# A selective scan that spreads B in fp32, with zero products in TensorE's gaps and fewer products on VectorE

## The chip, the cores and the metric

The kernel runs on one core of a Trainium2 chip. The metric is the time of one execution on the device, in microseconds (us). A core has TensorE (PE, matrix products into PSUM; PEld is its weight load), VectorE (DVE), ScalarE (ACT), GpSimd (POOL) and SyncE (SP), which here only issues transfers. The engines run beside each other and wait for each other through semaphores.

## The reference

The network takes x of shape 4 x 56 x 56 x 96 through two layers that hold a selective scan (a state-space model, run along the image in four directions) and then two attention layers. The scan takes nearly all of the time. For each image and direction, with 192 channels d, 16 states n and 3136 tokens t:

```python
dt   = softplus(...)                    # per token and channel
d_a  = exp(dt[..., None] * a)           # decay, per token, channel and state
d_b  = dt[..., None] * b_ssm[:, :, None, :]

def step(h, inp):
    da_t, db_t, x_t, c_t = inp
    h = da_t * h + db_t * x_t[..., None]     # the recurrence
    y_t = jnp.einsum('bds,bs->bd', h, c_t)   # sum over the states
    return (h, y_t)
```

The rows of B and C (`b_ssm`, `c_ssm`) and the input of dt are linear projections of the same token. Layer norms, convolutions, gates and small matrix products lie before, between and after the scans.

## The kernel before

Tokens are worked in chunks of 448. There are 2 layers x 4 images x 4 directions x 7 chunks = 224 chunks, and each chunk has 8 rounds: two halves `e` of the channels times four groups `q` of states, so 1792 rounds. In a round, 128 partitions hold 4 states x 32 channels, and three blocks `g` of 448 tokens hold the three groups of 32 channels.

The projection gives rows of C and B in 64 of 128 partitions, and a second copy of them in the other 64. GpSimd makes that copy the remainder beyond bf16, so that one bf16 product over 128 rows gives B nearly in fp32:

```python
def rows(self, ch):                      # ScalarE copies the projection out of PSUM
    ...
    ch.cf = sp.tile([128, CS], F32, name="cf")
    ...
def spread_b(self, ch, q):               # B of four states, on 32 partitions each
    ps = self.psum.tile([128, 512], F32, tag="b", name="b", bufs=1)[:, :CS]
    self.nc.tensor.matmul(ps, self.sel[:, q], self.upper(ch.cf), start=True, stop=True)
    return ps

def split(self, ch, n):                  # the remainder, in two parts, in rounds 1 and 2
    x = ch.cf[64 + 32 * n :]
    self.nc.gpsimd.tensor_tensor(x, x, self.upper(x), ALU.subtract)
```

`upper` is the high half of each fp32 word, read as bf16. `b` has one buffer, so the next B waits until VectorE's products have read the last one. A round, cut to what matters:

```python
def begin(n):
    ch, e, q = rounds[n]
    b = self.spread_b(ch, q)
    v = sp.tile([128, NG, CS + 2], F32, name="v", bufs=3)
    ahead = NQ * e + q not in (OWN_TAIL if ch.l and ch.i else OWN)
    if ahead:                            # GpSimd makes the third block's product
        nc.gpsimd.tensor_tensor(v[:, 2, TOKENS], ch.du[e][:, 2], ch.cb[q][:, 1], ALU.mult)
    return b, v, ahead
...
for n, (ch, e, q) in enumerate(rounds):
    b, v, ahead = nxt
    for g in range(2 if ahead else 3):   # VectorE makes two products, or all three
        nc.vector.tensor_tensor(v[:, g, TOKENS], ch.du[e][:, g], b, ALU.mult)
    self.prepare(ch, nexts.get(ch), r)   # parts of the next chunk
    ...
    yield "C", n, r                      # side work: the other layers' pieces
    nxt = begin(n + 1)
    if len(late) == 2:
        self.add_up(*late.pop(0))        # the sum over states, two rounds late
    self.prepare_ahead(afters.get(ch), r)
    for g in range(NG):
        ...                              # before g == 2: more side work
        nc.vector.tensor_tensor_scan(    # the recurrence of 448 tokens
            v[:, g, way], da[g][:, way], v[:, g, way], 0.0, ALU.mult, ALU.add)
        ...
        decay(n + 1, g)                  # ScalarE: exp(dt * a) of the next round into PSUM
    hc = sp.tile([128, NG, CS], F32, name="hc", bufs=3)
    nc.gpsimd.tensor_tensor(hc, v[:, :, TOKENS],   # h times C
        ch.cb[q][:, 0].unsqueeze(1).to_broadcast([128, NG, CS]), ALU.mult)
    late.append((ch, e, q, hc))
```

`add_up` sums over the four states of a partition group with four matrix products of 32 columns each (the fourth is a spare whose rows are not used):

```python
for n, g in enumerate((0, 1, 2, 2)):
    nc.tensor.matmul(self.y[32 * n : 32 * n + 32], self.four, hc[:, g], start=n == 3, stop=n == 3 or q == NQ - 1)
```

`OWN = (3, 4, 6)` are the rounds of a chunk in which VectorE makes all three products; `OWN_TAIL = (3, 4)` replaces it in the second layer from the second image on. Side work (norms, convolutions, gates, attention of the other images) is cut into pieces, and each piece goes into a round when an account of estimated ScalarE and TensorE time, `spend` and `room`, has room for it. The order of instructions on each engine is fixed when the program is built.

Of the kernel before, what the change touches and what calls it, by code (L numbers as in the profile page):

```python
# [11 lines left out]
F32 = mybir.dt.float32  # L12
F16 = mybir.dt.float16
BF16 = mybir.dt.bfloat16
F8 = mybir.dt.float8e5
AF = mybir.ActivationFunctionType
ALU = mybir.AluOpType
# [5 lines left out]
C = 96  # L23
DI = 192
NS = 16
NE = 2
NG = 3
NQ = 4
# [7 lines left out]
RANK = (12, 6)  # L36
NW, LATE_NW = 13, 20
NWIN = 3
OWN = (3, 4, 6)
OWN_TAIL = (3, 4)  # L40

SPARE = (1.2, 3.0)
# [2 lines left out]
BANKS, LATE_BANKS = 2, 4  # L45
DEPTH, LATE_DEPTH = 3, 6

ORDER = (((0, 0), (0, 1), (1, 0), (1, 1)), ((0, 1), (1, 0), (1, 1), (0, 0)))
WD = NE * 128 + NE * C + NE + NE * NQ * NG

# [29 lines left out]
def lay_out(i):  # L82
    i = {k: np.asarray(v) for k, v in i.items()}
    c96, c128, w96, w128, q96, q128 = Cols(C), Cols(128), Cols(C), Cols(128), Cols(C), Cols(128)
    p0, p1 = "L0_conv_", "L1_conv_"

    for n in ("norm_w", "norm_b", "norm2_w", "norm2_b", "ffn_b2"):
        c96.add("0" + n, i[p0 + n][:, None])
    for n in (
        "dw_b bn1_g bn1_b bn1_m bn1_v pw_b bn2_g bn2_b bn2_m bn2_v ln_g ln_b fus_b fus_ln_g fus_ln_b"  # L90
    ).split():
        c96.add("1" + n, i[p1 + n][:, None])
    c96.add("1dw_w", i[p1 + "dw_w"].reshape(C, 9))
    for l in "23":
        c96.add(l + "bq", i[f"L{l}_attn_bqkv"][:C, None])
        c96.add(l + "bff", i[f"L{l}_attn_bff"][:, None])
        c96.add(l + "b2", i[f"L{l}_ffn_b2"][:, None])
        c128.add(l + "b1", i[f"L{l}_ffn_b1"].reshape(3, 128).T)

    scan = (  # L100
        (i[p0 + "ssm_xw"], i[p0 + "ssm_dtw"], i[p0 + "ssm_dtb"], i[p0 + "ssm_Alog"], i[p0 + "ssm_D"]),
        (
            i[p1 + "x_proj_w"],
            i[p1 + "dt_w"],
            i[p1 + "dt_b"],
            i[p1 + "A_logs"].reshape(4, DI, NS),
            i[p1 + "Ds"].reshape(4, DI),
        ),
    )
    wd = np.zeros((2, 4, 128, WD), np.float32)  # L110
    for l, (xw, dw, db, al, dd) in enumerate(scan):
        r = RANK[l]
        for k in range(4):
            t = xw[k].T
            m = np.zeros((128, NE, 2, 64), np.float32)
            m[:C, :, 0, :32] = np.concatenate([t[:, r + NS :], t[:, r : r + NS]], 1).reshape(NE, C, 32).swapaxes(0, 1)
            m[:C, :, 0, 32 : 32 + r] = t[:, :r].reshape(NE, C, r).swapaxes(0, 1)
            m[:, :, 1, :32] = m[:, :, 1, 32:] = m[:, :, 0, :32]
            wt = np.zeros((128, DI), np.float32)
            wt[32 : 32 + r] = dw[k].T  # L120
            bias = np.zeros((128, NE), np.float32)
            bias[:C] = db[k].reshape(NE, C).T
            a = al[k].reshape(NE, NG, 32, 4, NQ).transpose(3, 2, 0, 4, 1).reshape(128, -1)
            wd[l, k] = np.concatenate([m.reshape(128, -1), wt, bias, a], 1)
        c128.add(f"{l}D", dd.T.reshape(NE, C, 4).swapaxes(0, 1))
    c128.add("0dir", np.broadcast_to(i[p0 + "dir_w"], (128, 4)))
    c128.add("0b1", i[p0 + "ffn_b1"].reshape(3, 128).T)
    for n, v in (
        ("1conv_b", i[p1 + "conv_b"][:, None]),
        ("1conv_w", i[p1 + "conv_w"].reshape(DI, 9)),  # L130
        ("1g", i[p1 + "out_norm_g"][:, None]),
        ("1b", i[p1 + "out_norm_b"][:, None]),
    ):
        c128.add(n + "a", v[:128])
        c128.add(n + "b", v[128:])

    w96.add("0in", _in_blocks(i[p0 + "in_w"].T))
    w96.add("1in", _in_blocks(i[p1 + "in_proj_w"].T))
    w96.add("0w1", i[p0 + "ffn_w1"].T)
    w96.add("1pw", i[p1 + "pw_w"])  # L140
    f = i[p1 + "fus_w"].T
    w96.add("1fa", f[:C])
    w96.add("1fb", f[C:])
    w96.add("1out", i[p1 + "out_proj_w"])
    w = i[p0 + "out_w"].T
    w128.add("0outa", w[:128])
    w128.add("0outb", w[128:])
    w128.add("0w2", i[p0 + "ffn_w2"].T.reshape(3, 128, C).transpose(1, 0, 2))
    for l in "23":
        w96.add(l + "qkv", i[f"L{l}_attn_Wqkv"])  # L150
        w96.add(l + "ff", i[f"L{l}_attn_Wff"])
        q96.add(l + "w1", i[f"L{l}_ffn_W1"].T)
        q128.add(l + "w2", i[f"L{l}_ffn_W2"].T.reshape(3, 128, C).transpose(1, 0, 2))
    bqkv = np.stack([i[f"L{l}_attn_bqkv"] for l in "23"])
    cols = {"c96": c96, "c128": c128, "w96": w96, "w128": w128, "q96": q96, "q128": q128}
    arrays = {"x": np.ascontiguousarray(i["x"]).reshape(NB, L, C), "bqkv": bqkv, "wd": wd}
    arrays.update({k: v.array() for k, v in cols.items()})
    return arrays, {k: v.at for k, v in cols.items()}


class Net:
    def __init__(self, ctx, tc, aps, at, out):
# [10 lines left out]
        self.ready = set()  # L173
        self.held, self.lend, self.live, self.g = 0, 0, [], {}
        self.backlog, self.limit, self.paced = [0.0, 0.0], ACT_LIMIT, False
        self.U = [self.big.tile([C, L], F32, name=f"U{e}") for e in range(NE)]
        self.Y = [self.big.tile([C, L], F32, name=f"Y{e}") for e in range(NE)]
        self.wp = pool("work", bufs=2)
# [63 lines left out]
    def setup(self):  # L242
# [94 lines left out]
        self.b2q = const.tile([C, 2], F32, name="b2q")  # L337
        with tc.tile_pool(name="stage", bufs=1) as st:

            self.sel = const.tile([128, NQ, 128], BF16, name="sel")  # L340
            parts = st.tile([128, 128], F32, name="parts")
            nc.vector.tensor_tensor(parts[:, :32], self.ident[:, 64:96], self.ident[:, 96:], ALU.add)
            nc.vector.tensor_tensor(parts[:, :32], parts[:, :32], self.ident[:, :32], ALU.add)
            for q in range(NQ):
                nc.vector.tensor_copy(
                    self.sel[:, q].rearrange("p (s d) -> p s d", s=4),
                    parts[:, NS + q : NS + q + 13 : 4].unsqueeze(2).to_broadcast([128, 4, 32]),
                )
            t = st.tile([C, 2, 3, 128], F32, name="q96")
            nc.scalar.dma_start(t.rearrange("p l m f -> p (l m f)"), self.aps["q96"])  # L350
            nc.vector.tensor_copy(self.w1q, t, saturate=False)
# [64 lines left out]
    def project_step(self, ch, e):  # L416

        if e == 0:
            ch.ps = self.pp()
        self.nc.tensor.matmul(  # L420
            ch.ps.rearrange("p (a b) -> p a b", b=HS), ch.par.wx[:, e],
            self.in_order(self.U[e], ch.orient, ch.c * CS, CS), start=e == 0, stop=e == NE - 1,
        )

    def parameters(self, ch):

        nc, sp = self.nc, self.sp
        if ch.step == 0:
            self.p = p = Step()
            wd = sp.tile([128, WD], F32, name="wd")  # L430
            nc.sync.dma_start(wd, self.aps["wd"][ch.l, ch.k])
            a = NE * 128
            p.wx = wd[:C, :a].rearrange("p (e m) -> p e m", e=NE)
            p.wt = wd[:, a : a + NE * C]
            a += NE * C
            p.dtb = wd[:C, a : a + NE]
            p.alog = wd[:, a + NE :]
            p.na = sp.tile([128, NE, NQ, NG], F32, name="na")
            p.carry = sp.tile([128, NE, NQ, NG], F32, name="carry")
        ch.par = self.p  # L440
# [10 lines left out]
    def rows(self, ch):  # L451
        nc, sp, p = self.nc, self.sp, ch.par
        if ch.step == 0:
            na = p.na.rearrange("p e q g -> p (e q g)")
            nc.scalar.activation(na, p.alog, AF.Exp)
            nc.scalar.mul(na, na, -1.0)
        ch.cf = sp.tile([128, CS], F32, name="cf")
        if ch.l == 0:
            nc.scalar.activation(ch.cf, ch.ps, AF.Copy, scale=self.cscale[:, ch.k : ch.k + 1])  # L459
        else:  # L460
            nc.scalar.copy(ch.cf, ch.ps)

# [56 lines left out]
    def prepare(self, ch, follow, r):  # L519
# [8 lines left out]
            self.rows(follow)  # L528
        elif r == 1:
            self.step_sizes(follow)  # L530
            self.split(follow, 0)
        elif r == 2:
            self.softplus(follow)
            self.split(follow, 1)
        elif r == 3:
            self.times_u(follow, 0)
            for e in range(NE):
# [21 lines left out]
    def spread_b(self, ch, q):  # L559

        ps = self.psum.tile([128, 512], F32, tag="b", name="b", bufs=1)[:, :CS]
        self.nc.tensor.matmul(ps, self.sel[:, q], self.upper(ch.cf), start=True, stop=True)  # L562
        return ps

    def upper(self, x):

        return x.bitcast(BF16).rearrange("p (t h) -> p t h", h=2)[:, :, 1]

    def split(self, ch, n):

        x = ch.cf[64 + 32 * n :]
        self.nc.gpsimd.tensor_tensor(x, x, self.upper(x), ALU.subtract)  # L575

    def scans(self):

# [115 lines left out]
    def add_up(self, ch, e, q, hc):  # L694

        nc = self.nc
        if q == 0:
            self.y = self.psum.tile([128, 512], F32, tag="y", name="y", bufs=1)[:, :CS]
            o = self.y[:C].rearrange("p (a b) -> p a b", b=HS)
            a, w = (self.U[e], self.skip[ch.l][:, e]) if ch.skip else (self.Y[e], self.ident[:C, :C])  # L700
            nc.tensor.matmul(o, w, self.in_order(a, ch.orient, ch.c * CS, CS), start=True, stop=False)  # L701

        for n, g in enumerate((0, 1, 2, 2)):
            nc.tensor.matmul(  # L704
# [167 lines left out]
            yield  # L872

    def spend(self, act, pe):
        self.backlog = [a + b for a, b in zip(self.backlog, (act, pe))]

    def half_round(self):
# [397 lines left out]
```

## Time and profile before

| | |
|---|---|
| time, median of 3 | 9206.25 us (9201.96 to 9231.71) |
| span of the profiled execution | 9215.2 us |
| mean granted TensorE clock | 0.733 |
| transfers | 1417 MB, 154 GB/s |

Its costliest groups, in the page's form (line, engine, operation, what is written and read, count, then busy us and mean ns of one, then the idle time just before them and what ended most of it):

```profile
L687 POOL TENSOR_TENSOR hc<-v,cb 128x1344 f32<-128x1344 f32 x1792 | 5154.2, 2877 | 619.7 <-DVE v L677 304.7
L677 DVE TENSOR_TENSOR_SCAN v<-da,v 128x449 f32<-128x449 f32 (+1 forms) x5376 | 5480.6, 1071 | 166.3 <-ACT da L624 68.6
L624 ACT ACTIVATE da<-dt,na 128x448 f32<-128x448 f32 x5376 | 3407.4, 638 | 1851.5 <-DVE v L677 1808.7
L704 PE MATMUL y<-hc,four 128*32 128x448 f32 x14336 | 2319.9, 729 | 4.3 <-POOL hc L687 4.0
L562 PE MATMUL b<-cf,sel 128*128 128x448 bf16 x1792 | 809.5, 452 | 814.0 <-DVE v L652 812.0
```

An fp32 product stands in the records as two instructions. The page also gives the busy share of each engine in 40 equal slices of the span, a digit for tenths, and PEclk, the share of full speed that TensorE's clock was granted in the slice.

### The profile page before, as it was taken

The numbers are of one execution on the slowest core, as the hardware profiler recorded it, in microseconds if no ns is written. First come the engines' busy times: TensorE is split into PE (matmuls) and PEld (weight loads), VectorE is DVE, ScalarE is ACT, GpSimd is POOL, SyncE is SP. The second block draws the span as 40 slices with busy tenths as digits, with TensorE's granted clock in tenths as the row PEclk, the third lists the DMA queues.
The fourth block names the chain that finished last, engine by engine and source line by source line (L and its number), as shares of the span: only waits on it lengthen the run. The fifth ranks groups of instructions, "written<-read, shape, count | busy, mean of one in ns | idle before, by whom it ended". The sixth has DMA issues, their size and how long they took to land. (4 is left out here: it accounts for less than half of the span.)

```text
span 9215.2 us, 110220 instructions
## 1 busy us (share of the span) xinstructions
PE 7255.3 (79%) x28342; PEld 2367.6 (26%) x28342; DVE 7878.4 (85%) x10197; ACT 6155.2 (67%) x12259; POOL 7816.4 (85%) x4320
## 2 busy tenths in 40 slices
PE   6777677787778777876778768887888788987887
PEld 2222122221222122221222113322233222322244
DVE  5998988899888998989888997899878998888951
ACT  5777667676777667766776655577755776666645
POOL 5888988899888988889888898899878998888951
PEclk7777677776787677866777667776777777876786
DMA  5666666667666676667656675566755666665631
GB/s 150 171 172 167 169 164 158 154 164 185 153 160 150 162 177 159 164 144 173 170 147 157 154 181 141 129 159 155 178 133 139 156 167 170 148 147 132 163 87 41
DMA packets 951297, 1417.21 MB, mean 154 GB/s; under 512 B 176578, under 2 KB 943812, under 8 KB 949796
## 3 DMA queue, kind: packets, MB, share of 16 engines
q1 hardware_dynamic: 949888, 1408.37, 62.4%
q8 instruction: 223, 3.65, 0.2%
q14 instruction: 414, 3.39, 0.1%
q10 hardware_dynamic: 772, 1.80, 0.1%
HBM read 1141.42 MB, written 268.14 MB: 153 GB/s over the span
## 5 line engine op out<-in xcount | busy, mean ns | idle before, releaser
L687 POOL TENSOR_TENSOR hc<-v,cb 128x1344 f32<-128x1344 f32 x1792 | 5154.2, 2877 | 619.7 <-DVE v L677 304.7
L677 DVE TENSOR_TENSOR_SCAN v<-da,v 128x449 f32<-128x449 f32 (+1 forms) x5376 | 5480.6, 1071 | 166.3 <-ACT da L624 68.6
L624 ACT ACTIVATE da<-dt,na 128x448 f32<-128x448 f32 x5376 | 3407.4, 638 | 1851.5 <-DVE v L677 1808.7
L652 DVE TENSOR_TENSOR v<-du,b 128x448 f32<-128x448 f32 x4172 | 2341.0, 608 | 770.0 <-PE b L562 626.4
L704 PE MATMUL y<-hc,four 128*32 128x448 f32 x14336 | 2319.9, 729 | 4.3 <-POOL hc L687 4.0
L562 PE MATMUL b<-cf,sel 128*128 128x448 bf16 x1792 | 809.5, 452 | 814.0 <-DVE v L652 812.0
L632 POOL TENSOR_TENSOR v<-du,cb 128x448 f32<-128x448 f32 x1204 | 1368.5, 1137 | 81.0 <-DMA cb<-cd 57.3
L704 PEld LDWEIGHTS y<-hc,four 128*32 128x32 f32 x14336 | 319.3, 123 | 1802.8 <-issue 1101.0
L420 PE MATMUL pp<-U,wd 96*128 96x448 f32 x896 | 701.8, 871 | 10.0 <-DMA U<-u 9.9
L751 POOL TENSOR_TENSOR rs<-rs,power 112x4 f32<-112x4 f32 x252 | 253.9, 1008 | 532.8 <-ACT rs L750 341.8
L831 PE MATMUL ps<-win,dg 64*64 64x220 f32 (+10 forms) x1962 | 598.7, 516 | 64.8 <-ACT dtc L485 47.1
L701 PE MATMUL y<-Y,ident 96*96 96x448 f32 x672 | 585.2, 964 | 4.7 <-ACT carry L681 3.0
L491 POOL TENSOR_TENSOR duc<-dtc,U 96x448 f32<-96x448 f32 x448 | 557.0, 1243 | 2.5 <-ACT dtc L485 2.5
L711 ACT COPY Y<-y 96x448 f32<-96x448 f32 x448 | 339.8, 758 | 269.3 <-PE y L704 268.3
L624 ACT ACT_TABLE_LOAD x385 | 494.0, 1283 | 14.7 <-DMA dt<-dd 8.0
L562 PEld LDWEIGHTS <-sel 128*128 128x128 bf16 x1792 | 208.8, 117 | 951.7 <-issue 948.7
L575 POOL TENSOR_TENSOR cf<-cf 64x448 f32<-64x448 f32 x448 | 417.0, 931 | 38.1 <-ACT cf L459 3.0
L755 PE MATMUL ps<-ident,rs 112*96 112x112 f32 x1752 | 304.1, 337 | 181.2 <-POOL rs L751 100.1
L729 PE MATMUL ps<-w,cen 96*96 96x448 f32 x448 | 281.1, 730 | 169.1 <-DVE w L1093 42.8
L681 ACT COPY carry<-v 128x3 f32<-128x3 f32 x1536 | 295.8, 193 | 171.0 <-DVE v L677 168.9
L747 PE MATMUL ps<-avg,w 96*112 96x1 f32 (+2 forms) x1976 | 295.6, 267 | 96.1 <-ACT w L784 46.8
L831 PEld LDWEIGHTS ps<-win,dg 64*64 64x64 f32 (+2 forms) x1962 | 248.6, 178 | 451.9 <-issue 321.2
(411 smaller groups left out, 6328.9 us busy)
## 6 DMA issues: line engine op xcount, KB each, us to landing
cb<-cd SPq DMA_DIRECT2D x3584, 112.0 KB, 4.0
dt<-dd SPq DMA_DIRECT2D x1792, 168.0 KB, 4.2
du<-dd SPq DMA_DIRECT2D x1792, 168.0 KB, 4.0
dd<-dtc SPq DMA_DIRECT2D x448, 168.0 KB, 2.0
dd<-duc SPq DMA_DIRECT2D x448, 168.0 KB, 2.0
U<-u SPq DMA_DIRECT2D x112, 168.0 KB, 4.7
z<-w SPq DMA_DIRECT2D x56, 224.0 KB, 3.6
u<-w SPq DMA_DIRECT2D x56, 224.0 KB, 2.9
```

The source lines that it names most:

```text
L420: self.nc.tensor.matmul(ch.ps.rearrange("p (a b) -> p a b", b=HS), ch.par.wx[:, e], self.in_order(self.U[e], ch.orient, ch.c * CS, CS), st ...
L491: self.nc.gpsimd.tensor_tensor(du.rearrange("p (a b) -> p a b", b=HS), ch.dtc[e].rearrange("p (a b) -> p a b", b=HS), self.in_order(self.U ...
L562: self.nc.tensor.matmul(ps, self.sel[:, q], self.upper(ch.cf), start=True, stop=True)
L575: self.nc.gpsimd.tensor_tensor(x, x, self.upper(x), ALU.subtract)
L624: nc.scalar.activation(da[g][:, TOKENS], ch.dt[e][:, g], AF.Exp, scale=ch.par.na[:, e, q, g : g + 1])
L632: nc.gpsimd.tensor_tensor(v[:, 2, TOKENS], ch.du[e][:, 2], ch.cb[q][:, 1], ALU.mult)
L652: nc.vector.tensor_tensor(v[:, g, TOKENS], ch.du[e][:, g], b, ALU.mult)
L677: nc.vector.tensor_tensor_scan(v[:, g, way], da[g][:, way], v[:, g, way], 0.0, ALU.mult, ALU.add)
L687: nc.gpsimd.tensor_tensor(hc, v[:, :, TOKENS], ch.cb[q][:, 0].unsqueeze(1).to_broadcast([128, NG, CS]), ALU.mult)
L701: nc.tensor.matmul(o, w, self.in_order(a, ch.orient, ch.c * CS, CS), start=True, stop=False)
L704: nc.tensor.matmul(self.y[32 * n : 32 * n + 32], self.four, hc[:, g], start=n == 3, stop=n == 3 or q == NQ - 1,)
L831: self.nc.tensor.matmul(o[:, a - r0 : e - r0, x0:x1], diag[:, tap], win[:, a + dy - lo : e + dy - lo, x0 + dx : x1 + dx], start=n == 0, st ...
```

## The change

It has four parts. B is spread by an fp32 product over 64 rows, in place of a bf16 product over 128 rows that held the split. The subtractions on GpSimd that made the split are gone, and the projection makes 64 rows in place of 128. VectorE makes all three products in two rounds of eight everywhere, in place of three in the first layer and the second layer's first image; GpSimd makes the others. And before each sum over states, TensorE gets products of a weight tile of zeros with a fixed tile of data, which add nothing to `y`. Their number follows from an account: where the side work of the last round is estimated at less than `WARM` = 1.5 us, the rest is filled at 0.19 us each, so none to eight. They are meant to keep TensorE busy[...].

```diff
-OWN = (3, 4, 6)
+OWN = (3, 4)
...
+WARM, FILL, PER_P = 1.5, 0.19, 0.58
...
-            self.sel = const.tile([128, NQ, 128], BF16, name="sel")
...
+            self.sel = const.tile([64, NQ, 128], F32, name="sel")
...
+            self.some = self.upper(self.tiles["w128"][:, :CS])
+            self.zeros = const.tile([128, C], BF16, name="zeros")
+            nc.vector.memset(self.zeros, 0.0)
...
-            ch.ps = self.pp()
+            ch.ps = self.pp()[:64]
...
-        ch.cf = sp.tile([128, CS], F32, name="cf")
+        ch.cf = sp.tile([64, CS], F32, name="cf")
...
         elif r == 1:
             self.step_sizes(follow)
-            self.split(follow, 0)
         elif r == 2:
             self.softplus(follow)
-            self.split(follow, 1)
...
-        self.nc.tensor.matmul(ps, self.sel[:, q], self.upper(ch.cf), start=True, stop=True)
+        self.nc.tensor.matmul(ps, self.sel[:, q], ch.cf, start=True, stop=True)
...
+        for _ in range(int(max(0.0, WARM - self.work) / FILL + 0.5)):
+            nc.tensor.matmul(self.y[:C], self.zeros, self.some, start=False, stop=False)
+        self.work = 0.0
 
         for n, g in enumerate((0, 1, 2, 2)):
...
     def spend(self, act, pe):
+        self.work += PER_P * pe
         self.backlog = [a + b for a, b in zip(self.backlog, (act, pe))]
```

The cuts leave out the layout of the projection's weights, which loses its second copy, and the start value of the account.

More of the change, by code (lines that the diff above doesn't have):

```diff
@@ L46 @@
 DEPTH, LATE_DEPTH = 3, 6
+WARM, FILL, PER_P = 1.5, 0.19, 0.58
 ORDER = (((0, 0), (0, 1), (1, 0), (1, 1)), ((0, 1), (1, 0), (1, 1), (0, 0)))
-WD = NE * 128 + NE * C + NE + NE * NQ * NG
+WD = NE * 64 + NE * C + NE + NE * NQ * NG
 class Cols:
@@ L114, in lay_out @@
             t = xw[k].T
[L115 to L118, printed above, removed]
+            m = np.zeros((128, NE, 64), np.float32)
+            m[:C, :, :32] = np.concatenate([t[:, r + NS :], t[:, r : r + NS]], 1).reshape(NE, C, 32).swapaxes(0, 1)
+            m[:C, :, 32 : 32 + r] = t[:, :r].reshape(NE, C, r).swapaxes(0, 1)
             wt = np.zeros((128, DI), np.float32)
@@ L338, in setup @@
         with tc.tile_pool(name="stage", bufs=1) as st:
-            self.sel = const.tile([128, NQ, 128], BF16, name="sel")
-            parts = st.tile([128, 128], F32, name="parts")
-            nc.vector.tensor_tensor(parts[:, :32], self.ident[:, 64:96], self.ident[:, 96:], ALU.add)
-            nc.vector.tensor_tensor(parts[:, :32], parts[:, :32], self.ident[:, :32], ALU.add)
+            self.sel = const.tile([64, NQ, 128], F32, name="sel")
             for q in range(NQ):
@@ L346, in setup @@
                     self.sel[:, q].rearrange("p (s d) -> p s d", s=4),
-                    parts[:, NS + q : NS + q + 13 : 4].unsqueeze(2).to_broadcast([128, 4, 32]),
+                    self.ident[:64, NS + q : NS + q + 13 : 4].unsqueeze(2).to_broadcast([64, 4, 32]),
                 )
+            self.some = self.upper(self.tiles["w128"][:, :CS])
+            self.zeros = const.tile([128, C], BF16, name="zeros")
+            nc.vector.memset(self.zeros, 0.0)
             t = st.tile([C, 2, 3, 128], F32, name="q96")
@@ L431, in parameters @@
             nc.sync.dma_start(wd, self.aps["wd"][ch.l, ch.k])
-            a = NE * 128
+            a = NE * 64
             p.wx = wd[:C, :a].rearrange("p (e m) -> p e m", e=NE)
@@ L456, in rows @@
             nc.scalar.mul(na, na, -1.0)
-        ch.cf = sp.tile([128, CS], F32, name="cf")
+        ch.cf = sp.tile([64, CS], F32, name="cf")
         if ch.l == 0:
-            nc.scalar.activation(ch.cf, ch.ps, AF.Copy, scale=self.cscale[:, ch.k : ch.k + 1])
+            nc.scalar.activation(ch.cf, ch.ps, AF.Copy, scale=self.cscale[:64, ch.k : ch.k + 1])
         else:
@@ L567, in upper @@
         return x.bitcast(BF16).rearrange("p (t h) -> p t h", h=2)[:, :, 1]
-    def split(self, ch, n):
-        x = ch.cf[64 + 32 * n :]
-        self.nc.gpsimd.tensor_tensor(x, x, self.upper(x), ALU.subtract)
     def scans(self):
@@ L701, in add_up @@
             nc.tensor.matmul(o, w, self.in_order(a, ch.orient, ch.c * CS, CS), start=True, stop=False)
+        for _ in range(int(max(0.0, WARM - self.work) / FILL + 0.5)):
+            nc.tensor.matmul(self.y[:C], self.zeros, self.some, start=False, stop=False)
+        self.work = 0.0
         for n, g in enumerate((0, 1, 2, 2)):
```

## The prediction

> **What bounds the kernel now.** I read the first two parts of the page, then the list of waits, then groups, then stretches, then TensorE's order of instructions in a slow and a fast stretch.
>
> ```profile
> PE 7255.3 (79%) x28342; PEld 2367.6 (26%) x28342; DVE 7878.4 (85%) x10197; ACT 6155.2 (67%) x12259; POOL 7816.4 (85%) x4320
> DVE  5998988899888998989888997899878998888951
> PEclk7777677776787677866777667776777777876786
> ```
>
> VectorE is the busiest engine, GpSimd is beside it, and TensorE's clock is granted only to about seven tenths. VectorE's first product from B starts at 112 us and its last at 8853; what lies outside is other work. From VectorE's busy time and span, 9215.2 - 7878.4 = 1337 us are idle. Stretches of the trace give about 76 us of it before 95 us, 949 between 95 and 8800, 311 after. The middle 949 is what a change can reach. Who ends it:
>
> ```profile
> PE b L562 <- DVE v L652: 812.0, 487, 13.3
> DVE v L652 <- PE b L562: 626.4, 412, 5.3
> ```
>
> Each round, TensorE spreads B into one PSUM bank, VectorE multiplies from it, and only then may TensorE write the next B there. 487 times TensorE was early and waited; 412 times it was late and VectorE stood for 626 us, two thirds of the reachable idle time. Why is it late?
>
> ```profile
> 4001.00:4022.00 21.00, 21.00 (x72) 5.81 (x71) 15.71 (x21) 8.35 (x20) 15.75 (x9) 0.50 0.76 172
> 4100.00:4200.00 100.00, 70.14 (x251) 13.77 (x250) 99.88 (x129) 64.12 (x127) 97.29 (x51) 0.63 0.65 161
> 4440.00:4450.00 10.00, 7.51 (x37) 2.16 (x37) 9.23 (x12) 8.24 (x15) 8.78 (x5) 1.00 0.93 206
> ```
>
> The columns are the stretch, its length, busy PE, PEld, DVE, ACT, POOL, then TensorE's granted clock. In the first, TensorE never rests, at half clock, and VectorE works 15.71 of 21 us. In the second TensorE has little to do, and VectorE is full (99.88) even at clock 0.63. So a slow clock hurts only where TensorE is loaded, and without a late B VectorE can run at nearly 100%. TensorE in the first and third stretch (start, length):
>
> ```profile
> 4008.40 0.56 PE L562 MATMUL b<-cf,sel 128*128 128x448 bf16 x1
> 4008.89 1.72 PE L704 MATMUL y<-hc,four 128*32 128x448 f32 x8
> 4010.54 1.99 PE L420 MATMUL pp<-U,wd 96*128 96x448 f32 x2
> 4012.46 2.48 PE L831 MATMUL ps<-win,dg 64*64 64x220 f32 x12
> 4014.87 0.56 PE L562 MATMUL b<-cf,sel 128*128 128x448 bf16 x1
> ...
> 4443.60 0.36 PE L562 MATMUL b<-cf,sel 128*128 128x448 bf16 x1
> 4443.89 0.96 PE L704 MATMUL y<-hc,four 128*32 128x448 f32 x8
> 4444.78 1.02 PE L420 MATMUL pp<-U,wd 96*128 96x448 f32 x2
> 4445.64 0.36 PE L562 MATMUL b<-cf,sel 128*128 128x448 bf16 x1
> ```
>
> At half clock B comes 6.47 us after B (4014.87 - 4008.40), with a convolution between; at full clock the same y takes 0.96 instead of 1.72 and pp 1.02 instead of 1.99. In the timeline VectorE's products start at 4089.95, 4093.97, 4097.98 and 4101.99 us, so a round with two products takes 4.0 us; the next start, after a round with three, is 4106.64, or 4.65. So at half clock TensorE is the slower engine in a loaded round, and at full clock it is not.
>
> [...] The trace has just 0.50 and 1.00 in short stretches[...]. [...] 21 us of unbroken busy time stayed at 0.50, so a busy row in the profile is not yet activity that counts. [...]
>
> **The change part by part.**
>
> ```profile
> L652 DVE TENSOR_TENSOR v<-du,b 128x448 f32<-128x448 f32 x4172 | 2341.0, 608 | 770.0 <-PE b L562 626.4
> L632 POOL TENSOR_TENSOR v<-du,cb 128x448 f32<-128x448 f32 x1204 | 1368.5, 1137 | 81.0 <-DMA cb<-cd 57.3
> L575 POOL TENSOR_TENSOR cf<-cf 64x448 f32<-64x448 f32 x448 | 417.0, 931 | 38.1 <-ACT cf L459 3.0
> ```
>
> *VectorE's rounds, three to two of eight.* The built program has 4032 VectorE products for 4172, and 1344 on GpSimd for 1204: 140 move. VectorE loses 140 x 0.608 = 85 us, busy 7878 to 7793. It is on the path: -85.
>
> *GpSimd.* It gains 140 x 1.137 = 159 us and loses the 448 subtractions, 417 us: busy 7816 to 7558, 97% of VectorE's. It comes off the path that it nearly shared; I count nothing more.
>
> *B in fp32.* [...] The pp pair's pitch gives 0.86 us for 0.29 (4443.89 - 4443.60) at full clock, 1.9 for 0.5 at half. TensorE gains 1792 x 0.57 = 1.02 ms of work at full clock. A B that is late is later by 0.6 us or more; one that is early costs nothing, as VectorE scans for about 3.05 us after the products that free the bank.
>
> *Zeros.* The built program holds 4795 of them: none in 885 rounds, eight in 374, four in 340, other numbers in the rest, mean 2.7 a round. At 0.2 us each[...] that is 0.54 us a round, 0.96 ms in all. They lie in TensorE's idle time if the clock is full.
>
> *The clock.* TensorE's work in a round at full clock: y 0.89 (4444.78 - 4443.89), B 0.86, zeros 0.54, and the rest. The rest is 7255 - 2320 (y) - 810 (B) = 4125 us at the mean clock of 0.733, so about 0.73 x 4125 = 3000; less some 300 in the tail, 2700 / 1792 = 1.5. Sum 3.8 us in a round of about 4.5, or 84% at full clock; before, 0.89 + 0.29 + 1.5 = 2.7 in 4.9, or 55%, and it fell back all the time. At half clock the new sum would be 7.6 us, more than a round, so TensorE would stream without a pause[...]. I expect a granted clock of 0.90 to 0.97 between 100 and 8850 us; start and tail have no zeros and stay.
>
> *Late Bs.* They need a lag over 3.05 - 1.0 = 2 us. Most of the 626 us fell in half-clock windows. With a nearly steady clock I leave 200 us, for rounds with dense side work, the six tenths that each late B costs more, and a few half-clock windows that are now heavier: -425. The other waits in the middle (about 320 us: decays, GpSimd products, transfers) partly grow as VectorE presses harder and partly go with the two engines' relief: -20.
>
> *Sum.* 9206 - 85 - 425 - 20 = 8676; I say 8680, -5.7%.
>
> **The rivals.**
>
> *The zeros do not earn the clock.* Zero weights[...] leave the clock at 0.73. Then a round of TensorE is 3.8 / 0.73 = 5.2 us, longer than VectorE's; 1792 x 5.2 + 112 + 358 = 9790 us, slower by 6%. For it: the 21 busy us at half clock. Against it: y's weights are mostly zeros too and run in the full-clock stretches, the moving operand here is real weights, and the fp32 B alone adds activity.
>
> *GpSimd becomes the bound.* With hc at 2.88 and one product at 1.14 a round of it is 4.02 us, exactly VectorE's 4.0, for six rounds running, and the factors' powers (1.0 us each) come on top. It catches up only in two rounds. For it: POOL 97.29 in the full stretch above. Against it: that stretch still held the subtractions, and three v buffers let it lag by a round. It would cost 50 to 150 us: about 8800.
>
> *Another wait takes B's place.* ScalarE's decays sit behind table loads, and the transfers' share (0.65 in the middle) rises in crowded stretches. It would eat half of the gain: 8900 to 8950.
>
> **Range and chances.** The product and GpSimd terms are sure; the 425 may be 250 to 550 and the rivals lie mostly above, so 8500 to 8920. Faster by 2% means under 9022: only the first rival, or two together, would prevent it. 0.88 faster, 0.07 within 2%, 0.05 slower.
>
> **What would show it.** Right: PEclk digits of 9 in the middle, TensorE busy near 85 to 90%, the wait of VectorE for B below 250 us, VectorE at 89 to 91% of a shorter span, B near 1.0 us in its row, GpSimd near 7560. Wrong: PEclk still 7 with B's wait above 626 us (first rival); waits of scans for GpSimd's v, or of products for hc, above 150 us (second); decays or transfers at the head of VectorE's waits (third).

## The result, and the profile after

The changed kernel takes 10361.14 us (median of 4 runs, 10338.47 to 10376.03) against 9217.49 for the kernel before in the same sessions: a ratio of 1.124, 95% interval 1.121 to 1.127. It is slower by an eighth.

From the page of the changed kernel, its busy times, TensorE's clock in slices, and two groups (the two figures between the bars are busy us and mean ns of one):

```profile
PE 9476.3 (91%) x34929; PEld 3165.4 (31%) x34929; DVE 7858.5 (76%) x10056; ACT 6150.6 (59%) x12259; POOL 7561.5 (73%) x4012
...
PEclk8887988988888988899788987878777778786886
...
L563 PE MATMUL b<-cf,sel 64*128 64x448 f32 x3584 | 2134.4, 680 | 160.9 <-DVE v L645 160.6
...
L696 PE MATMUL y<-w,zeros 128*96 128x448 bf16 x4795 | 1294.4, 407 | 0.0
```

From its list of waits (us in total, times, longest):

```profile
DVE v L645 <- PE b L563: 1544.0, 773, 6.7
```

TensorE is busy 91% of the span and has become the bound. It waits 161 us for VectorE's products in place of 812, and VectorE waits 1544 us for B in place of 626. VectorE's and GpSimd's busy times did not grow. The clock did rise, from 0.733 to 0.829, but not to full, and in the second half of the span 7 is as common a digit as 8.

One stretch of the program shows where the time goes: the 24 rounds from the 131st B on, found in three traces by counting B's products. First the kernel before:

```profile
719.04:838.11 119.07, 94.31 (x350) 29.61 (x350) 104.36 (x133) 93.67 (x180) 101.90 (x55) 0.76 0.68 170
```

The changed kernel:

```profile
787.33:934.53 147.20, 137.16 (x426) 40.14 (x426) 103.13 (x129) 93.73 (x180) 99.22 (x51) 0.74 0.55 135
```

And an experiment told below, the changed kernel with its fp32 B over 128 rows:

```profile
728.57:855.22 126.65, 108.48 (x428) 36.49 (x427) 103.52 (x130) 93.74 (x181) 99.41 (x52) 0.91 0.62 155
```

The columns are the stretch, its length, busy PE, PEld, DVE, ACT, POOL, the granted clock, then the DMA share and GB/s. VectorE works 103 to 104 us in each. The changed kernel needs 28 us more for it than the kernel before, at clock 0.74, with TensorE busy 137 of 147 us. With 128 rows, the same list of products is done at 0.91, and 20.5 of the 28 us are gone.

TensorE in the changed kernel, just ahead of that stretch (start, length):

```profile
778.91 1.86 PE L563 MATMUL b<-cf,sel 64*128 64x448 f32 x2
780.70 1.73 PE L696 MATMUL y<-w,zeros 128*96 128x448 bf16 x4
782.36 1.72 PE L700 MATMUL y<-hc,four 128*32 128x448 f32 x8
784.01 1.80 PE L475 MATMUL pp<-cf,wd 12*96 12x448 f32 x2
785.75 1.66 PE L743 MATMUL ps<-avg,w 96*112 96x1 f32 x8
787.33 1.86 PE L563 MATMUL b<-cf,sel 64*128 64x448 f32 x2
```

The same round with B over 128 rows:

```profile
724.32 0.92 PE L567 MATMUL b<-cf,sel 128*128 128x448 f32 x2
725.07 0.95 PE L700 MATMUL y<-w,zeros 128*96 128x448 bf16 x4
725.96 0.96 PE L704 MATMUL y<-hc,four 128*32 128x448 f32 x8
726.85 0.99 PE L479 MATMUL pp<-cf,wd 12*96 12x448 f32 x2
727.76 0.95 PE L747 MATMUL ps<-avg,w 96*112 96x1 f32 x8
728.57 1.00 PE L567 MATMUL b<-cf,sel 128*128 128x448 f32 x2
```

B comes 8.42 us after B in the first and 4.25 in the second; VectorE needs 4.0 for a round with two products. In both, one product starts as another ends, without a gap. The first stays at half clock all the same (0.50 from 778.91 to 787.33, TensorE busy throughout).

### The profile page after: what moved, and what is told of

It reads as the page before. It is cut to its first block, busy times and chain, and to the rows that moved or that the text cites. A ratio compares the mean times of both kernels' runs of the same rounds, so it can differ in the third digit from the quotient of the medians.

```text
span 10373.7 us, 122887 instructions
## 1 busy us (share of the span) xinstructions
PE 9476.3 (91%) x34929; PEld 3165.4 (31%) x34929; DVE 7858.5 (76%) x10056; ACT 6150.6 (59%) x12259; POOL 7561.5 (73%) x4012
## 5 line engine op out<-in xcount | busy, mean ns | idle before, releaser
L645 DVE TENSOR_TENSOR v<-du,b 128x448 f32<-128x448 f32 x4032 | 2280.8, 612 | 1832.5 <-PE b L563 1544.0
L563 PE MATMUL b<-cf,sel 64*128 64x448 f32 x3584 | 2134.4, 680 | 160.9 <-DVE v L645 160.6
L700 PE MATMUL y<-hc,four 128*32 128x448 f32 x14336 | 2054.8, 650 | 0.0
L625 POOL TENSOR_TENSOR v<-du,cb 128x448 f32<-128x448 f32 x1344 | 1528.7, 1137 | 50.5 <-DMA cb<-cd 43.9
L696 PE MATMUL y<-w,zeros 128*96 128x448 bf16 x4795 | 1294.4, 407 | 0.0
L563 PEld LDWEIGHTS b<-cf,sel 64*128 64x128 f32 x3584 | 612.1, 210 | 1361.2 <-issue 466.7
L696 PEld LDWEIGHTS <-zeros 128*96 128x96 bf16 x4795 | 584.6, 134 | 992.5 <-issue 801.1
L423 PE MATMUL pp<-U,wd 96*64 96x448 f32 x896 | 674.9, 842 | 4.5 <-DMA U<-u 4.5
```

Source lines behind the costliest of these rows:

```text
L423: self.nc.tensor.matmul(ch.ps.rearrange("p (a b) -> p a b", b=HS), ch.par.wx[:, e], self.in_order(self.U[e], ch.orient, ch.c * CS, CS), st ...
L563: self.nc.tensor.matmul(ps, self.sel[:, q], ch.cf, start=True, stop=True)
L696: nc.tensor.matmul(self.y[:C], self.zeros, self.some, start=False, stop=False)
```

## The experiments

Three theories stood after the result. *Load*: fp32 B and zeros are more work than TensorE's gaps hold. *Clock*: fp32 B over 64 rows does not hold the clock up, so the clock falls under it. *Order*: the zeros stand ahead of y and the next B in TensorE's order and delay them.

**Zeros taken out.**

```diff
-WARM, FILL, PER_P = 1.5, 0.19, 0.58
+WARM, FILL, PER_P = 0.0, 0.19, 0.58
```

> The changed kernel with no zero products (4795 fewer, 1.29 ms of TensorE's busy row); B stays fp32 over 64 rows and VectorE keeps two rounds of eight. Load theory (fp32 B and zeros are both more work than TensorE's gaps hold, and each is late in turn): TensorE loses a good third of what was added, time near 9800, mean clock falls from 0.83 to about 0.75. Order theory (the zeros stand ahead of y and the next B in a strict queue, and that is nearly all of the loss): 9250 or less. Clock theory (fp32 B over 64 rows does not count as activity, the zeros alone hold the clock up): clock at 0.70 or less and time at 10300 or more.

10424 us, ratio to the kernel before 1.129 (1.124 to 1.134), clock 0.693. That is 63 us more than with the zeros, though the two intervals still touch, and a lower clock than the kernel before had.

```profile
PE 9538.9 (91%) x30134; PEld 2866.6 (27%) x30134; DVE 7857.5 (75%) x10056; ACT 6147.9 (59%) x12259; POOL 7550.3 (72%) x4012
```

This is the page of the run without zeros. With 4795 products less, TensorE is busy no less than with them (9539 against 9476 us): the work that was saved was lost again, at the lower clock. The zeros are not the loss, and only the clock theory expected this.

**bf16 B brought back**, with the split and the subtractions; zeros and VectorE's two rounds stay.

```diff
-        self.nc.tensor.matmul(ps, self.sel[:, q], ch.cf, start=True, stop=True)
+        self.nc.tensor.matmul(ps, self.sel[:, q], self.upper(ch.cf), start=True, stop=True)
```

> The kernel before with bf16 B over 128 split rows and GpSimd's subtractions, plus the 4795 zero products and VectorE's two rounds: the changed kernel with its B part undone. Load theory: TensorE loses 1.0 ms of work at full clock, the larger half, time 9000 to 9400. Clock theory: clock at 0.92 or more in the scan part, VectorE's wait for B below 300 us, time 8800 or less, although GpSimd now carries both the subtractions and the third products (its busy time 7976). Order theory: the zeros still stand in the queue, time 10000 or more.

9124 us, ratio 0.990 (0.987 to 0.992), clock 0.865. Its list of waits has

```profile
DVE v L657 <- PE b L567: 541.1, 363, 6.6
```

so the whole slowdown hangs on the fp32 B. The time is in the load theory's range; clock and time rose and fell less than the clock theory said.

**fp32 B over 128 rows.** The tile of B's rows and the selecting weights get 64 more rows, all zeros. The number of products and their columns stay as they were.

```diff
-            self.sel = const.tile([64, NQ, 128], F32, name="sel")
+            self.sel = const.tile([128, NQ, 128], F32, name="sel")
...
-        ch.cf = sp.tile([64, CS], F32, name="cf")
+        ch.cf = self.cfs[self.turn]        # two tiles of 128 rows, the upper 64 zeroed once
+        self.turn = 1 - self.turn
```

> The changed kernel with the fp32 B over 128 rows, of which 64 are zeros in both operands: the same number of passes and columns, twice the active rows. Load and order theories: same time as the changed kernel, 10361 within 1%, clock 0.83 as there. Clock theory: the product with twice the rows counts as more activity, clock at 0.88 or more, time 10000 or less.

9458 us, ratio 1.026 (1.024 to 1.028), clock 0.922: 904 us less than the changed kernel, for adding rows of zeros. Its page and its list of waits:

```profile
PE 8314.1 (88%) x34929; PEld 3053.9 (32%) x34929; DVE 7829.1 (83%) x10058; ACT 6146.1 (65%) x12259; POOL 7553.2 (80%) x4012
```

```profile
DVE v L649 <- PE b L567: 885.7, 554, 5.9
```

The same 34929 products keep TensorE busy 1162 us less. The clock theory stands. What is left, 885.7 us of waiting at clock 0.92, is mostly load: against bf16 B with zeros, fp32 B costs 9458 - 9124 = 334 us, even with GpSimd's subtractions gone; TensorE is busy with B for 1917.5 us in place of 723.8.

**VectorE's two rounds alone**, in the kernel before.

```diff
-OWN = (3, 4, 6)
+OWN = (3, 4)
```

> The kernel before with only VectorE's rounds changed, two of eight everywhere; the subtractions stay on GpSimd, whose busy time becomes 7816 + 159 = 7975, above VectorE's 7793. All theories: no part of the slowdown is here. If VectorE binds, 85 us less, 9130; if GpSimd binds in its six rounds running, 9200 to 9300.

9208 us, ratio 0.998 (0.997 to 0.999): 16 us faster. It is not part of the slowdown.

**The product that gives dt over 128 rows too**, in the kernel with B over 128 rows.

```diff
-        rows = slice(32, 32 + RANK[ch.l])
+        rows = slice(0, 128)
```

> The kernel with fp32 B over 128 rows and zeros, and also the product that gives dt (12 or 6 rows, 448 of them) over all 128 rows, the added ones zeros: no more passes or columns. Clock theory in the form that active rows are what counts: the clock rises from 0.92 to 0.95 or more, time 9250 to 9400. If only the B product was special: 9458 within 0.5%.

9349 us, ratio 1.013 (1.011 to 1.016), clock 0.936: 109 us less by rows of zeros in a product that is a quarter as frequent as B. So B is not the only product whose rows mattered here. The product itself also became shorter, 0.829 us to the next start at full clock in place of 0.917 (medians), so not all of the 109 us need be the clock.

**B over 128 rows, zeros taken out.**

```diff
-WARM, FILL, PER_P = 1.5, 0.19, 0.58
+WARM, FILL, PER_P = 0.0, 0.19, 0.58
```

> fp32 B over 128 rows, without the zero products. If the zeros are mostly a load and an obstacle in the queue: faster than the 9458 with them, 9200 to 9350. If they are needed for the clock here too: clock falls from 0.92 to about 0.80, time 9500 to 9700. With 64 rows the zeros were worth 63 us.

9343 us, ratio 1.013 (1.011 to 1.015), clock 0.868. Once B has 128 rows, the zeros cost 114 us: the clock falls by 0.054 without them, and it is still faster.

**bf16 B, zeros, dt over 64 rows** in place of 12 or 6, and VectorE's three rounds.

```diff
-        rows = slice(32, 32 + RANK[ch.l])
+        rows = slice(0, 64)
```

> bf16 B over 128 split rows, zeros, VectorE's three rounds as before, and the dt product over 64 rows in place of 12 or 6. Against 9124 with zeros and two rounds of VectorE: clock from 0.865 to 0.89, time 9000 to 9080 if rows count in proportion; 9124 within 0.3% if 64 rows do not count.

9115 us, ratio 0.990 (0.985 to 0.994), clock 0.874. 9 us less than 9124 is within the interval: 64 rows for dt showed no gain here, though VectorE's third round was put back at the same time.

**The same with the zeros behind y**, but for each fourth round.

```diff
+        if q == NQ - 1:
+            self.fill(fill)
         for n, g in enumerate((0, 1, 2, 2)):
...
+        if q < NQ - 1:
+            self.fill(fill)
```

> The same with the zeros behind the sum over states instead of ahead of it, but for each fourth round, where they would stand before the copy of y. Order theory: the sums and what hangs on them come up to 1.7 us earlier, VectorE's waits for decays and carries fall, 50 us or more under the run with zeros ahead. Clock theory alone: the same time within 0.3%, as the number of zeros is the same.

9121 us, ratio 0.989 (0.987 to 0.992), clock 0.871: the same. The order theory falls, at least with bf16 B, where I tried it.

**fp32 B over 96 rows.**

```diff
-        self.nc.tensor.matmul(ps, self.sel[:, q], ch.cf, start=True, stop=True)
+        self.nc.tensor.matmul(ps, self.sel[:96, q], ch.cf[:96], start=True, stop=True)
```

> The changed kernel with fp32 B over 96 rows, 32 of them zeros: between 64 rows (10361, clock 0.83) and 128 rows (9458, clock 0.92). Active rows in proportion: 9700 to 10050, clock 0.86 to 0.90. A step between 64 and 96 rows: within 1% of 9458. A step between 96 and 128: within 1% of 10361.

9609 us, ratio 1.042 (1.041 to 1.044), clock 0.896. It lies between and nearer to 128 rows. The clock is in the range given for proportion and the time below it: both follow the number of rows, but the time not in proportion, and neither in one step.

**Zeros over 32 rows**, in the kernel with bf16 B and zeros.

```diff
-            nc.tensor.matmul(self.y[:C], self.zeros, self.some, start=False, stop=False)
+            nc.tensor.matmul(self.y[:C], self.zeros[:32], self.some[:32], start=False, stop=False)
```

> The kernel with bf16 B and zeros (9124, clock 0.865), its 4795 zero products over 32 rows in place of 128: same columns, same time in the queue. Row theory: they no longer count, clock back to 0.74 or less (0.739 without zeros), and as they are still work, time 9250 to 9500. If any busy time counts and only the fp32 B is special: 9124 within 0.5%, clock 0.86.

9888 us, ratio 1.072 (1.067 to 1.077), clock 0.708. From its list of waits:

```profile
DVE v L657 <- PE b L567: 1014.5, 610, 5.3
DVE v L682 <- ACT da L629: 382.6, 239, 4.2
```

TensorE in it, at half clock (start, length):

```profile
4716.52 1.72 PE L709 MATMUL y<-w,zeros 32*96 32x448 bf16 x4
4718.18 1.72 PE L713 MATMUL y<-hc,four 128*32 128x448 f32 x8
```

Four zero products over 32 rows take 1.66 us to the next start, as four over 128 rows did at half clock (780.70 to 782.36 above): only the rows changed, not the length. With bf16 B throughout, these 4795 products rebuild two thirds of the changed kernel's loss of 1144 us: 763 us. VectorE waits 1015 us for B in place of 541, and 383 for decays in place of 90. The zeros over 128 rows had earned their place by their rows; over 32 they are only work, and the clock is below that of no zeros at all (0.739). The row theory's clock came as expected; the time is well above its 9500.

**B and dt over 128 rows, no zeros.**

```diff
-WARM, FILL, PER_P = 1.5, 0.19, 0.58
+WARM, FILL, PER_P = 0.0, 0.19, 0.58
...
-        rows = slice(32, 32 + RANK[ch.l])
+        rows = slice(0, 128)
```

> fp32 B and the dt product over 128 rows, without zeros. Rows for dt brought 109 us with zeros and no zeros brought 114 with B over 128 rows. If both add: about 9230, that is the time of the kernel before within 0.5%, clock 0.89. If the passes of fp32 bind TensorE whatever its clock: 9300 or more, with VectorE waiting 800 us or more for B.

9228 us, ratio 1.001 (1.000 to 1.002), clock 0.890. Both gains add, and fp32 B then costs nothing against the kernel before. It gains nothing either: VectorE still waits

```profile
DVE v L649 <- PE b L567: 803.6, 513, 6.3
```

so fp32 B remains a load even at clock 0.89.

**bf16 B with a third of the zeros** (1552), dt over 64 rows, three rounds of VectorE.

```diff
-WARM, FILL, PER_P = 1.5, 0.19, 0.58
+WARM, FILL, PER_P = 0.75, 0.19, 0.58
```

> bf16 B, dt over 64 rows, VectorE's three rounds, and 1552 zeros in place of 4795 (the account asks for 0.75 us in place of 1.5). If the zeros are more load than help here too: 9050 to 9090. If each earns its place through the clock: clock 0.79 to 0.82, time 9150 to 9200, half way back to the kernel before.

9125 us, ratio 0.990 (0.988 to 0.992), clock 0.812. That is between the two forecasts, and the same time as with 4795 zeros at clock 0.874: with bf16 B, more zeros raise the clock and give it back as work. The four kernels with bf16 B and zeros over 128 rows beat the kernel before by 1%, and cannot be told apart.

One more count, from eight of the traces. In the traces the clock is 0.50 or 1.00, and a stretch of either lasts a whole number of times 3.41 us (all 790 stretches of the kernel before and all 632 of the changed kernel, but for the last of each; the shortest is 3.41). I took the windows of that grid at half clock in which TensorE's row was busy for at least 97%, and asked how many were followed by a window at full clock:

```
kernel                       B             zeros      clock   full-busy half-clock windows, share followed by full clock
no_zeros                     fp32  64      none       0.693   1357   0.22
zeros_32_rows                bf16 128      32 rows    0.708   1324   0.23
changed kernel               fp32  64      128 rows   0.829    871   0.36
kernel before                bf16 128      none       0.733    667   0.57
b_96_rows                    fp32  96      128 rows   0.896    439   0.65
bf16b_zeros                  bf16 128      128 rows   0.865    496   0.68
b128_no_zeros                fp32 128      none       0.868    455   0.78
b_128_rows                   fp32 128      128 rows   0.922    293   0.83
```

At the same busy row, the chance of the full clock runs from 0.22 to 0.83. With zeros over 128 rows it is 0.36, 0.65 and 0.83 for fp32 B over 64, 96 and 128 rows; with bf16 B it is 0.68 and 0.23 for zeros over 128 and 32.

The windows themselves show how the rows entered. Let each product count, from its start to the next start, by its active rows over 128, and take a window's mean. Of these 5902 windows, 1555 have a mean under 0.70, and not one was followed by full clock; of the 1222 between 0.70 and 0.80 it was 0.12; of the 2279 between 0.80 and 0.90 it was 0.68; of the 846 with 0.90 or more, 0.975. In each of the eight runs alone none under 0.70 led to full clock, and at least 0.93 of those from 0.90 did.

## Why the prediction was wrong

*The step that failed.* I wrote that at half clock "TensorE would stream without a pause", and took it that this brings the clock to 0.90 to 0.97. That was an assumption, which no trace showed. Where it was loaded, TensorE did stream without a pause, and did not get the full clock: in the changed kernel a fully busy half-clock window led to full clock in 0.36 of cases, less than before (0.57). The clock from 95 to 9980 us was 0.83. The sign had been on the table: 21 us of unbroken busy time at 0.50 (with a mean of active rows of 0.69, counted as above), and my own remark that a busy row is not yet activity that counts. I applied it to the zeros, as a rival, and not to the new B, which went from 128 active rows to 64 and from 0.292 to 0.946 us to the next start at full clock. In these runs a busy array was not enough, and the clock went with the active rows: of the fully busy half-clock windows above, 0 of 1555 with a mean under 0.70 and 0.975 of the 846 with 0.90 or more were followed by full clock.

*The sum, term by term.*
- Late Bs, predicted 200 us: 1544. Two mistakes are in it. One is the 64 rows: against 128 they made 904 us of the time and 658 of this wait (1544 - 886), through the clock and through a longer B, 0.946 us at full clock where I had taken 0.86 from a product over 96 rows. The other is load: at clock 0.92 the wait is still 886 us. A mean of 84% busy says little of a loaded stretch, where B stands behind side work in TensorE's order (8.42 us from B to B above) and is late although the mean has room; bf16 B with the same zeros waits 541.
- Products with zeros, predicted to lie in idle time and earn the clock: the clock rose with them, zero weights or not (0.739 without and 0.865 with them, at bf16 B). The 0.2 us for each was an estimate; in the changed kernel it is 0.198 us to the next start at full clock and 0.374 at half (medians). With B over 64 rows they brought nothing clear (63 us, with intervals that touch), with B over 128 they cost 114, and with bf16 B they brought 9208 - 9124 = 84 us against VectorE's two rounds alone.
- VectorE's two rounds, predicted 85 us: 16 us when alone. VectorE was busy 66 us less there (7812 against 7878), but its waits for B grew from 626 to 663 us and those for GpSimd's products from 63 to 79.
- GpSimd, predicted 7558 us busy: 7561.5. The removal of the subtractions freed GpSimd as worked out. What that brought in time no run shows, as none takes the subtractions out alone.

*The rivals.* The first had the direction right and half of the size (9790, "slower by 6%"), and the wrong culprit: it was not the zeros that failed to raise the clock. What it held against itself, that "the fp32 B alone adds activity", was the mistake: without zeros the fp32 B over 64 rows gave clock 0.693. The second did not come: VectorE's longest wait for GpSimd is 69 us, for hc. Of the third, decays cost VectorE 152 us in place of 69, a small part.

*What remains open.* Between 64 and 96 rows two things change at once: the clock, and the product itself, which takes 0.946 us from start to next start at full clock over 64 rows and 0.856 over 96 or 128. Of the 752 us between those two runs I cannot say how much is the one and how much the other; an estimate from 1792 Bs, 0.09 us each at full clock (0.946 - 0.856) and up to 0.3 at half (1.79 - 1.52), is 160 to 540 us of TensorE's time. Between 96 and 128 rows the product has the same median length, 0.856 us to the next start at full clock and 1.52 at half, so the 151 us are put down to the clock. The zeros over 32 rows show the clock's effect (0.865 to 0.708, and 763 us) without any change to B or to the products' length. I did not try real data in place of the added zeros, nor the number of columns.

## What to carry to other kernels

Before a product is traded for another, compare not only number and columns but active rows: here B over 64 rows left TensorE's row 91% busy at clock 0.829, where B over 128 rows had 0.922, and the 904 us between them are more than the product's own time (160 to 540 us, the estimate above), through all that ran beside it. Rows of zeros that filled an operand to 128 cost no time here and paid (those 904 us), while extra products with zeros were work as well: they brought 84 us with bf16 B and cost 114 with fp32 B over 128 rows. And a full TensorE row at half clock is a warning: more work of this kind may not bring the clock (in the changed kernel it came after 0.36 of such windows).

## What the runs showed of the hardware that was not expected

- In these runs the granted clock followed the active rows even where operands were zeros: 0.829, 0.896 and 0.922 with fp32 B over 64, 96 and 128 rows, the added rows zero in both operands; 0.865 and 0.708 with products of zero weights over 128 and 32 rows, at the same length. In eight runs no fully busy half-clock window with a mean of active rows under 0.70 of 128 was followed by full clock (0 of 1555).
- From a half-clock window with a full busy row, the chance of full clock in the next was 0.22 to 0.83; from a full-clock window with a full row, 0.88 to 0.98 in these eight runs. Falling back under load was rare here, and coming back was not sure.
- The fp32 B of 448 columns was shorter over 96 or 128 rows (0.856 us to the next start at full clock and 1.52 at half, medians of the runs with zeros) than over 64 (0.946 and 1.79). The product that gives dt took 0.917 over 12 or 6 rows and 0.829 over 128, at full clock.
